# First weight quarter of each batch as two halves in rows of 4 KB, in place of three pieces by chunk; eleven identity matmuls in place of nine

## The chip, the core and the metric

The kernel runs on one core of one Trainium2 chip. A core has TensorE (PE in the profile, with its weight loads shown apart as PEld), VectorE (DVE), ScalarE (ACT), GpSimd (POOL) and SyncE (SP), an on-chip memory of 128 partitions, and PSUM, the memory into which TensorE writes. The metric is the device time of one execution in microseconds (us), taken as the median of several runs. All data here is float32; a float32 matmul appears in the profile as two records, and so does an identity matmul.

## The reference

For each of eight batches, x (256 tokens by 1024) is multiplied with one of eight weight matrices, chosen by an index; the product y goes through a base layer and a routed low-rank layer, and x is added:

```python
y      = einsum('bsi,boi->bso', x, weight[adapter_ids])
base   = einsum('btd,od->bto', y, base_W) + base_b
probs  = softmax(einsum('btd,nd->btn', y, router_W) + router_b)
p, i   = top_k(probs, 8)
w      = sum of p over the chosen rows by expert_map[i]
h      = einsum('btd,erd->bter', y, A)
out    = x + base + einsum('bter,eor->bto', h * w, B) * 2.0
```

## The kernel before

The work has two phases. **Phase one** computes y batch by batch. The 1024 by 1024 weight is split in four quarters of 512 by 512 (1 MB each): a11, a12, a21, a22. Seven quarter products, made from the quarters and from sums and differences of them, take the place of eight. Each quarter product is a `block` of 16 matmuls: four output tiles m by four contraction chunks k of 128. **Phase two** does the same with the base layer over groups of four batches; the change leaves it alone.

A quarter lies on the chip as a tile "wt" of 128 partitions, 4 chunks k, 512 outputs: 8 KB a partition. There are eight such buffers (`wpool`, line 65), shared by the quarters, their sums and later operands.

`load(b)` (line 284) fetches batch b. For b = 0, x comes in two transfers of 512 KB on ACT's queue (line 302). All weights go on SP's queue, in program order: the adapter index is read into a register (line 307), then a11 in **three pieces** (lines 310 to 318): chunk 0 (256 KB), chunk 1 (256 KB), chunks 2 and 3 (512 KB). They come from a DRAM tensor of its own, `w11`, in which the host has laid each piece as one contiguous block, so that a row (one partition's contiguous run) is 2 KB in the first two pieces and 4 KB in the third. Then `load_w` (line 289) fetches a12, a22 and a21 from `wq`, where a quarter is stored as two contiguous halves of 512 KB with rows of 4 KB: for b = 0 in two transfers each (`parts = 2`), for later batches in one transfer of 1 MB.

The order on PE, DVE, ACT and SP is the order of the program text (`manual_schedule`). At the start PE runs nine identity matmuls (lines 363 to 365), which read nothing but a constant. DVE makes four differences of x (`turns`), then the sums of the weight quarters: s1 = a21 + a22 in two halves (line 342), s2 = s1 - a11 (347), s4 = a12 - s2 (350), a11 - a21 (351). PE runs the blocks of batch 0 in the order a11, a12, a22, s1, s2, s4, a11 - a21. For b = 0 the first five blocks go through their matmuls chunk by chunk (`k_outer`): all four m of k = 0, then of k = 1, and so on, so a block can begin when chunk 0 has landed. For b of 1 and more, `load(b + 1)` is issued at the top of batch b, and its blocks run one batch later. Each transfer into a wt buffer waits on SP until the buffer's earlier readers are done.

The accumulators of the first three blocks are called pa (a11), pb (a12) and, second buffer of the same name, pb again (a22); pc takes s1.

Of the kernel before, what the change touches and what calls it, by code (L numbers as in the profile page):

```python
# [10 lines left out]
F32 = mybir.dt.float32  # L11
# [17 lines left out]
def kernel(  # L29
# [3 lines left out]
    xq: bass.AP,  # L33
    xr: bass.AP,
    ids: bass.AP,
    w11: bass.AP,

    wq: bass.AP,
    bq: bass.AP,
    base_b: bass.AP,  # L40
# [6 lines left out]
    nc = tc.nc  # L47
    P = 128
# [2 lines left out]
    KC = 8  # L51
    KH = 4
    OH = 512
    NA = w11.shape[0]
    N = emap.shape[1]
    ER = bT.shape[0]
    E = (N + 1) // 2
# [7 lines left out]
    wpool = ctx.enter_context(tc.tile_pool(name="w", bufs=8))  # L65
# [141 lines left out]
    with ExitStack() as phase:  # L207
# [76 lines left out]
        def load(b):  # L284

            x = xpool.tile([P, 2, 2, KH, P], F32, name="x")
            q = {}

            def load_w(name, i, parts=1):
                q[name] = wpool.tile([P, KH, OH], F32, name="wt")  # L290
                t = q[name].rearrange("p (h k) o -> p h (k o)", h=2)
                for n in range(parts):
                    h = ts(n, 2 // parts)
                    nc.sync.dma_start(
                        t[:, h],
                        wq[ds(adapter, 1), i, h].rearrange("e h p f -> p (e h) f"),
                    )

            if b == 0:

                for j in range(2):
                    nc.scalar.dma_start(
                        x[:, j].rearrange("p i k t -> p (i k t)"), x0[j]
                    )
            else:
                nc.sync.dma_start(x.rearrange("p j i k t -> p (j i k t)"), xq[b - 1])
            adapter = nc.sync.value_load(
                ids_sb[0:1, b : b + 1], min_val=0, max_val=NA - 1
            )
            q["a11"] = wpool.tile([P, KH, OH], F32, name="wt")  # L310

            for k, n in ((0, 1), (1, 1), (2, 2)):
                nc.sync.dma_start(
                    q["a11"][:, ds(k, n)].rearrange("p k o -> p (k o)"),
                    w11[ds(adapter, 1), ds(k * P * OH, n * P * OH)].rearrange(
                        "e (p f) -> p (e f)", p=P
                    ),
                )
            parts = 2 if b == 0 else 1
            load_w("a12", 0, parts)  # L320
            load_w("a22", 2, parts)
            load_w("a21", 1, parts)
            return x, q

        def turns(x):
# [18 lines left out]
        def other_sums(q):  # L344
# [13 lines left out]
            tc.manual_schedule(engines={EN.PE, EN.DVE, EN.Activation, EN.SP})  # L358
        )
        x, q = load(0)  # L360
        first = q

        idle = ps_t.tile([P, S], F32, name="pt")
        for _ in range(9):
            nc.tensor.matmul(idle[:, :P], lhsT=ident, rhs=ident, start=True, stop=True)
        t1, t2, t4 = turns(x)
        first_sum(q)
# [2 lines left out]
        for b in range(B):  # L370
# [6 lines left out]
            if not last:  # L377
                x, nq = load(b + 1)
# [52 lines left out]
            if not last:  # L431
                other_sums(nq)
                q, t1, t2, t4 = nq, nt1, nt2, nt4
# [343 lines left out]
```

## Time and profile before

| what | value |
|---|---|
| median of 3 runs | 443.89 us (443.81 to 443.92) |
| the profiled execution | 442.66 us |
| its span, first to last instruction | 440.9 us |
| PE busy in the span | 434.5 us (99%), 2994 matmul records |
| DVE busy | 303.2 us (69%) |
| DMA traffic | 106.19 MB, mean 241 GB/s |
| granted TensorE clock | 1.00 in every stretch asked for |

The span runs from the first to the last instruction of the program; 1.76 us of the profiled execution lie outside it. Times inside the trace are in us from the span's start. PE's busy time is modelled from pipelined matmuls; the start times of its records are the sharper view.

The transfers that open the span, each with the time of its issue and of the semaphore update that tells of its landing, as the trace has them:

| transfer | KB | row | queue | issued | landed | after the landing before |
|---|---|---|---|---|---|---|
| x, first half | 512 | 4 KB | ACT | 0.74 | 4.05 | |
| x, second half | 512 | 4 KB | ACT | 1.15 | 5.31 | 1.27 |
| a11, chunk 0 | 256 | 2 KB | SP | 2.93 | 5.99 | |
| a11, chunk 1 | 256 | 2 KB | SP | 3.52 | 6.65 | 0.66 |
| a11, chunks 2 and 3 | 512 | 4 KB | SP | 4.05 | 8.79 | 2.15 |
| a12, first half | 512 | 4 KB | SP | 4.57 | 10.35 | 1.56 |
| a12, second half | 512 | 4 KB | SP | 5.31 | 11.64 | 1.29 |
| a22, first half | 512 | 4 KB | SP | 5.84 | 12.92 | 1.28 |
| a22, second half | 512 | 4 KB | SP | 6.36 | not shown | |
| a21, first half | 512 | 4 KB | SP | 7.08 | 15.48 | |
| a21, second half | 512 | 4 KB | SP | 7.68 | 16.74 | 1.26 |

In later batches the same three pieces of a11 appear with these landings: batch 1 20.77, 21.43, 22.69; batch 3 64.04, 64.67, 67.24; batch 4 93.08, 93.73, 96.40; batch 6 180.55, 181.28, 183.65.

### The profile page before, as it was taken

To read this page: it belongs to the slowest core of one execution; us is meant where nothing else is said; L and a number is where in the kernel's file an instruction comes from. 1 tells how busy PE (TensorE), PEld (TensorE's weight loads), DVE (VectorE), ACT (ScalarE), POOL (GpSimd) and SP (SyncE) were. 2 spreads that over 40 slices of the span, in tenths; PEclk is the share of its full clock that TensorE was granted. 3 is DMA by queue.
4 is the path that set the end of the run, shared out by engine and by line. 5 is a ranking of instruction groups with operands and counts; after the bars stand their busy time and mean duration, and the time that the engine had idled before them with its cause. 6 is when DMAs were issued, how large, how long until landed. Compare 5 with 4: busy or idle time off the path is not lost.

```text
span 440.9 us, 7299 instructions
## 1 busy us (share of the span) xinstructions
PE 434.5 (99%) x2994; PEld 409.7 (93%) x2994; DVE 303.2 (69%) x516; ACT 40.4 (9%) x89; POOL 0.7 (0%) x6
## 2 busy tenths in 40 slices
PE   7999999999999999999999999999999999999997
PEld 6999999999999999999999888888888888888886
DVE  2579695682963967939629957755597858755594
ACT  1101111011011110110111200000200200000200
POOL 0000000000000000000000000000000000000000
PEclk9999999999999999999999999999999999999999
DMA  8989879678597797893370956821967726921843
GB/s 303 407 348 349 313 273 273 219 282 308 181 284 274 240 290 266 266 315 143 134 297 0 371 226 238 337 115 37 354 249 261 277 89 214 371 83 53 306 153 133
DMA packets 34050, 106.19 MB, mean 241 GB/s; under 512 B 3298, under 2 KB 7138, under 8 KB 30818
## 3 DMA queue, kind: packets, MB, share of 16 engines
q1 hardware_dynamic: 33730, 104.69, 67.0%
q10 hardware_dynamic: 288, 1.05, 0.6%
q8 instruction: 23, 0.38, 0.3%
q14 instruction: 9, 0.07, 0.0%
HBM read 84.49 MB, written 21.23 MB: 240 GB/s over the span
## 4 chain that ended last, share of the span: by engine, by line
PE 92%; DVE 5%; DMA 1%; issue 1%; SPq 0%
PE pa L243 24%; PE pa L478 20%; PE pc L243 12%; PE pc L478 10%; PE pb L243 7%; PE ph L107 6%; PE pb L478 5%; PE pc L487 3%; PE pb L487 2%; PE pa L487 1%; DMA wt<-in_w_dram 1%; DVE tt L186 1%; PE pe L478 1%; DVE y L630 0%; PE pt L203 0%
## 5 line engine op out<-in xcount | busy, mean ns | idle before, releaser
L478 PE MATMUL pa<-tt,wt 128*128 128x256 f32 x324 | 78.0, 379 | 0.1
L478 PEld LDWEIGHTS pa<-tt,wt 128*128 128x128 f32 x324 | 61.4, 190 | 8.9 <-DVE u L508 0.5
L243 PE MATMUL pa<-x,wt 128*128 128x128 f32 x512 | 59.9, 275 | 1.8 <-DMA wt<-in_w_dram 1.8
L243 PEld LDWEIGHTS pa<-x,wt 128*128 128x128 f32 x512 | 58.5, 192 | 2.2 <-issue 1.3
L243 PE MATMUL pa<-tt,wt 128*128 128x128 f32 x480 | 56.0, 275 | 0.0
L243 PEld LDWEIGHTS pa<-tt,wt 128*128 128x128 f32 x480 | 54.8, 192 | 0.0
L116 DVE TENSOR_TENSOR lg<-ph,rb 128x30 f32<-128x30 f32 x8 | 1.5, 189 | 49.9 <-ACT h L115 49.9
L107 PE MATMUL ph<-ar_sb,y 128*128 128x143 f32 x256 | 32.7, 284 | 0.0
L107 PEld LDWEIGHTS ph<-ar_sb,y 128*128 128x128 f32 x256 | 31.8, 190 | 0.0
L243 PE MATMUL pc<-tt,wt 128*128 128x128 f32 x256 | 29.9, 275 | 0.0
L243 PE MATMUL pc<-x,wt 128*128 128x128 f32 x256 | 29.9, 275 | 0.0
L243 PE MATMUL pb<-x,wt 128*128 128x128 f32 x256 | 29.9, 275 | 0.0
L243 PEld LDWEIGHTS pc<-tt,wt 128*128 128x128 f32 x256 | 29.2, 192 | 0.0
L243 PEld LDWEIGHTS pc<-x,wt 128*128 128x128 f32 x256 | 29.2, 192 | 0.0
L243 PEld LDWEIGHTS pb<-x,wt 128*128 128x128 f32 x256 | 29.2, 192 | 0.0
L478 PE MATMUL pc<-tt,wt 128*128 128x256 f32 x112 | 27.8, 379 | 0.0
L342 DVE TENSOR_TENSOR wt<-wt 128x2048 f32<-128x2048 f32 (+1 forms) x9 | 18.5, 2051 | 10.2 <-DMA wt<-in_wq_dram 10.2
L478 PE MATMUL pc<-y,wt 128*128 128x256 f32 x96 | 24.0, 379 | 0.0
L478 PE MATMUL pb<-y,wt 128*128 128x256 f32 x96 | 24.0, 379 | 0.0
L478 PEld LDWEIGHTS pc<-tt,wt 128*128 128x128 f32 x112 | 21.2, 190 | 3.0
L478 PE MATMUL pa<-y,wt 128*128 128x256 f32 x92 | 21.9, 379 | 0.0
L601 DVE TENSOR_TENSOR q<-q,xt 128x512 f32<-128x512 f32 x31 | 21.3, 686 | 0.5
(117 smaller groups left out, 488.0 us busy)
## 6 DMA issues: line engine op xcount, KB each, us to landing
wt<-in_wq_dram SPq DMA_DIRECT2D x21, 1024.0 KB, 6.1
wt<-left_raw SPq DMA_DIRECT2D x14, 1024.0 KB, 5.5
wt<-left_sum SPq DMA_DIRECT2D x14, 768.0 KB, 8.0
xt<-in_xr_dram SPq DMA_DIRECT2D x32, 256.0 KB, 6.8
out_dram<-q SPq DMA_DIRECT2D x31, 256.0 KB, 2.3
x<-in_xq_dram SPq DMA_DIRECT2D x7, 1024.0 KB, 4.9
wt<-in_w_dram SPq DMA_DIRECT2D x16, 256.0 KB, 2.8
wt<-in_w_dram SPq DMA_DIRECT2D x8, 512.0 KB, 4.9
```

Of the source, the lines that this page charges most:

```text
L107: nc.tensor.matmul(ph[:, j], lhsT=y[:, k // KH, th, k % KH // 2, bi, k % 2, ts(j, P)], rhs=ar_sb[:, k, :], start=(j == order[0] and k == 0 ...
L116: nc.vector.tensor_add(lg, ph[:, :, ER:], rb.unsqueeze(1).to_broadcast([P, NTT, N]))
L186: nc.vector.tensor_sub(t[n], x, y)
L243: nc.tensor.matmul(acc[:, m // 2, m % 2, :], lhsT=left[:, k, ts(m, P)], rhs=right[:, k, :], start=(first and n == 0), stop=(k == KH - 1), ...
L342: nc.vector.tensor_add(q["s1"][:, h], q["a21"][:, h], q["a22"][:, h])
L478: nc.tensor.matmul(acc[mi][:, mi, :], lhsT=left[:, 2 * k + mi, :], rhs=right[:, k, :], start=(first and k == 0 and (mi == 0 or acc[0] is n ...
L487: nc.tensor.matmul(acc[mi][:, mi, :], lhsT=up[:, ts(mi, P)], rhs=hw, start=False, stop=True, skip_group_check=True,)
L601: add(q, q, x)
```

## The change

The tensor `w11` is gone. `wq` holds four quarters instead of three, all as two halves in rows of 4 KB, and a11 is loaded by `load_w` like the others: for batch 0 as two transfers of 512 KB, for each later batch as one of 1 MB. The bytes are the same. Nine identity matmuls become eleven. On the host side only the layout of the inputs changes.

```diff
-    NA = w11.shape[0]
+    NA = wq.shape[0]
...
-            q["a11"] = wpool.tile([P, KH, OH], F32, name="wt")
-
-            for k, n in ((0, 1), (1, 1), (2, 2)):
-                nc.sync.dma_start(
-                    q["a11"][:, ds(k, n)].rearrange("p k o -> p (k o)"),
-                    w11[ds(adapter, 1), ds(k * P * OH, n * P * OH)].rearrange(
-                        "e (p f) -> p (e f)", p=P
-                    ),
-                )
             parts = 2 if b == 0 else 1
-            load_w("a12", 0, parts)
-            load_w("a22", 2, parts)
-            load_w("a21", 1, parts)
+            load_w("a11", 0, parts)
+            load_w("a12", 1, parts)
+            load_w("a22", 3, parts)
+            load_w("a21", 2, parts)
...
-        for _ in range(9):
+        for _ in range(11):
             nc.tensor.matmul(idle[:, :P], lhsT=ident, rhs=ident, start=True, stop=True)
```

More of the change, by code (lines that the diff above doesn't have):

```diff
@@ L35 @@
     ids: bass.AP,
-    w11: bass.AP,
     wq: bass.AP,
@@ L740 @@
         "ids": a["itok_B_3_7"].reshape(1, nb),
-        "w11": _np.concatenate(
-            [w[:, 0, :2].reshape(len(w), -1)]
-            + [w[:, 0, 2:].transpose(0, 2, 1, 3).reshape(len(w), -1)],
-            axis=1,
-        ),
-        "wq": w[:, 1:]
-        .reshape(-1, 3, 2, d // 512, 128, d // 2)
+        "wq": w.reshape(-1, 4, 2, d // 512, 128, d // 2)
         .transpose(0, 1, 2, 4, 3, 5)
-        .reshape(-1, 3, 2, 128, d // 512 * (d // 2)),
+        .reshape(-1, 4, 2, 128, d // 512 * (d // 2)),
         "bq": base.reshape(4, 128, -1),
```

## The prediction

> **What bounds the kernel now.** I read the chain that ended last first, then what PE waited for, then the opening of PE's and SP's timelines, then each transfer's landing. The shares of the chain by engine, from the page:
>
> ```profile
> PE 92%; DVE 5%; DMA 1%; issue 1%; SPq 0%
> ```
>
> PE is the bound nearly everywhere. Everything PE ever waited for, over the whole span (us in total, times, longest):
>
> ```profile
> PE pa L243 <- DMA wt<-in_w_dram: 1.8, 2, 1.1
> PE pt L365 <- POOL ident masks.py:199: 1.4, 1, 1.4
> ```
>
> So the only waits that this change can touch are two, on pieces of a11. PE's timeline from 0 to 26 us (start, duration; the bracket is idle time before it) shows both:
>
> ```profile
> 1.36 3.63 PE L365 MATMUL pt<-ident 128*128 128x128 f32 x18 [1.36 <-POOL ident masks.py:199]
> 6.12 2.02 PE L243 MATMUL pa<-x,wt 128*128 128x128 f32 x16 [1.13 <-DMA wt<-in_w_dram]
> 8.84 2.05 PE L243 MATMUL pa<-x,wt 128*128 128x128 f32 x16 [0.69 <-DMA wt<-in_w_dram]
> 10.73 3.74 PE L243 MATMUL pb<-x,wt 128*128 128x128 f32 x32
> 14.30 3.74 PE L243 MATMUL pb<-tt,wt 128*128 128x128 f32 x32
> 17.87 3.74 PE L243 MATMUL pc<-tt,wt 128*128 128x128 f32 x32
> ```
>
> The identity matmuls end at 4.99, chunk 0 starts at 6.12, chunks 0 and 1 run through, then PE is idle 0.69 us until the third piece is there at 8.79. From 8.84 it never stops: the three starts after 10.73 lie 3.57 us apart, 32 records at 0.112. What counts is therefore one number, **the start of the second block (pb, a12), 10.73 now**; any shift of it moves the end by as much, unless a later wait appears. SP's timeline says when the transfers are issued:
>
> ```profile
> 2.93 1.46 SPq L313 DMA_DIRECT2D wt<-in_w_dram  x3
> 4.57 3.61 SPq L294 DMA_DIRECT2D wt<-in_wq_dram  x6
> ```
>
> **The two halves of batch 0.** Three issues on SP become two, and the followers are issued some 0.5 us sooner (2.93, 3.52, 4.05, 4.57 are the present steps). That by itself gains nothing: the trace's DMA packets show the first packet of a11 at 4.57, 1.6 us after its issue, when x's last packets (until about 4.9) still ran, and the engines stay full afterwards. The stream of bytes sets the landings, not SP.
>
> Half 1 is chunks 0 and 1 in one semaphore: 512 KB. Its bytes are those of the first two pieces, which had landed at 6.65. Per DMA engine they were 16 packets of 2 KB at 84 ns (1.34 us) and become 8 of 4 KB at 159 ns (1.27 us): 0.07 less, so 6.57. [...]
>
> [...] Five packets of the third piece took 0.76 to 1.18 us each; it landed 2.15 us after the second, where the later halves take 1.28. So the time of half 1 is the unknown cost, and rows for it are:
> - the a22 and second a12 halves: 1.28, no stall. Half 1 at 6.57.
> - a12's first half, the same form by the same line as the new half 1, the first of its tile: 1.56, a stall of 0.28. Half 1 at 6.85.
> - the third piece, the first in 4 KB rows on SP's queue: 2.15, a stall of 0.87. Half 1 at 7.44.
> - the third piece in batch 4 (93.73 to 96.40): 2.67, a stall of 1.39. Half 1 at 7.96.
>
> From there, PE: 0.13 us from landing to the first record (5.99 to 6.12), 16 records to chunk 2 in 1.86 (7.87 + 0.11 - 6.12), 16 more in 1.79 without a new start, 1.89 with one (10.73 - 8.84). I take a12's first half, the nearest in form and line: start 6.85 + 0.13 = 6.98, chunk 2 at 8.84. Half 2, at a12's second half's 1.29, lands at 8.14 and is not waited for; **pb starts at 8.84 + 1.79 = 10.63, 0.10 earlier**. If instead half 1 is clean and half 2 has the third piece's stall, half 2 lands at 6.57 + 2.15 = 8.72, PE restarts at 8.77, pb at 10.66: 0.07 earlier. Two distributions of one stall, the same answer: what PE loses by starting later (6.98 for 6.12) it had been losing anyway in the 0.69 us gap. Clean throughout: 6.70, 8.56, pb at 10.35: 0.38 earlier. That is about the most that can be won, since half 1 cannot land much before 6.57.
>
> Next in line behind it: a12's first half lands at 10.35 today and would now land at 8.14 + 1.28 = 9.4 to 10.35, before PE wants it in every case. DVE's s2 ends at 20.38 and is wanted at 21.45, s1's first half about 16.8 for 17.87: 1.07 us of room, more than the 0.38 that PE can come sooner.
>
> **The two added identity matmuls** are four records at 0.112 (the spacing from 4.27 on; before that it was 0.213): PE is done with them at 4.99 + 0.45 = 5.44, before 6.57. They cost nothing while half 1 lands after about 5.4, and cover part of the longer idle time: 6.98 - 5.44 = 1.54 us against 1.13 now. Would the matmuls slow down to the 0.213 spacing after such a pause? The row shows only that 1.13 us did not do it. From the row alone a longer pause could cost as much as the warm-up: 1.36 to 4.27 at 0.213 is 13.7 records, 1.4 us dearer than at 0.112. [...]
>
> **Later batches.** Seven times, three transfers become one of 1 MB, two SP issues fewer (0.53 us each). Hidden: batch 3's pieces land at 67.24 and are first read at 86.87 (DVE's s2) and 90.25 (PE). 20 us of cover, for a transfer that takes 5 to 6 us. Behind them on SP the next issue (64.86) waits for a block of PE, not for the queue. Should the 1 MB land 1 us later, the transfers after it have the same kind of slack. Zero.
>
> **Sum**: -0.10 us on the profiled execution, 442.66 to 442.56. The median of the runs lies 1.23 above it; the same shift on 443.89 gives **443.8**. About 0.2% (0.89 us) is what a measurement of this kernel can tell from no change.
>
> **Rivals.**
> 1. Clean stream, both halves at 1.28: -0.38, 443.5. For it: the five halves after a12's first run so. Against: each stream of 4 KB rows began with slow packets, x's too (eight of about 0.5 us). Still within 0.2%.
> 2. The stall moves wholly into half 1 at the third piece's size: 7.44, 7.57, 9.43, pb at 11.22: +0.49, 444.4. For it: half 1 is now the first in 4 KB rows on SP's queue. Against: it follows x, whose rows are 4 KB too, so the stream may be settled already. Within 0.2%.
> 3. Slower: the same mechanism at batch 4's size: half 1 at 7.96, PE 8.09, pb at 11.74: +1.01, 444.9. It decides from a landing of half 1 at 7.83 on (7.83 + 0.13 + 1.86 + 1.79 = 11.61, 0.89 late). Before, a stall behind chunks 0 and 1 was partly hidden by their 1.86 us of matmuls; a stall in half 1 has no work to hide behind. A clock that falls back in the pause would bring 2 to the same side. Against: the runs of before lie within 0.11 us of each other, so the opening is no lottery, and its own stall was 0.87.
> 4. Faster by over 0.2% would need pb at 9.84, half 1 at 6.05: 0.5 us sooner than its bytes can come. Only something outside the span could do it.
>
> **Chances**: the forecast (a stall of about 0.3 in half 1, or all in half 2) 0.45; rival 1 0.18; rival 2 0.20; rival 3 0.13; faster than 0.2% 0.04. So faster 0.04, same 0.83, slower 0.13. The range for 8 in 10 holds the first three cases with 0.2 to 0.3 for the runs: 443.3 to 444.6.
>
> **What would show it.** In the trace of after: one landing for half 1 near 6.6 to 6.9 and PE's first a11 record 0.13 later; all 32 a11 records without a gap (forecast), or with a gap before chunk 2 (the other distribution); 22 identity records ending near 5.4 with 0.112 spacing at the first real ones; pb near 10.6; no new wait of PE after it. The prediction is wrong if half 1 lands after 7.8, if the first a11 records are 0.213 apart, or if PE shows a wait in a later batch.

## The result, and the profile after

In the comparison of the two kernels, 20 runs each, the median fell from 443.75 to **442.78 us**; the ratio is 0.9983, with a 95% interval of 0.9976 to 0.9990. Three later comparisons, on three different chips, gave 0.9976 (0.9966 to 0.9986), 0.9984 (0.9976 to 0.9992) and 0.9981 (0.9971 to 0.9990). The medians differ by 0.97 us; the ratio follows the means, 443.66 and 442.91, and stands for a gain of 0.75 us. The 442.78 us lie below the predicted range of 443.3 to 444.6.

The profile after does not show it: that execution took 444.51 us, the longest of its 20, with a span of 442.7. Its chain of waits and what PE waited for, as shown for before:

```profile
PE 93%; DVE 5%; DMA 1%; issue 1%; SPq 0%
```

```profile
PE pa L241 <- DMA wt<-in_wq_dram: 1.9, 1, 1.9
PE pt L355 <- POOL ident masks.py:199: 1.4, 1, 1.4
```

PE's timeline from 0 to 20 us (lines 355 and 241 are 365 and 243 of before):

```profile
1.36 4.20 PE L355 MATMUL pt<-ident 128*128 128x128 f32 x22 [1.36 <-POOL ident masks.py:199]
7.42 5.44 PE L241 MATMUL pa<-x,wt 128*128 128x128 f32 x32 [1.86 <-DMA wt<-in_wq_dram]
12.69 3.74 PE L241 MATMUL pb<-x,wt 128*128 128x128 f32 x32
```

Half 1 landed at 7.28 and PE paused 1.86 us, longer than before; the gap ahead of chunk 2 is gone. But the 32 records of a11 took 5.44 us in place of some 3.7, and pb starts at 12.69. The view by stretches says why (stretch and length in us; busy time and count of PE, PEld, DVE, ACT and POOL; granted clock, DMA share, GB/s):

```profile
4.48:7.89 3.41, 1.55 (x14) 1.39 (x13) 1.71 (x3) 0.00 (x0) 0.00 (x0) 1.00 0.97 376
7.89:11.31 3.42, 3.42 (x18) 3.42 (x18) 0.97 (x2) 0.00 (x0) 0.00 (x0) 0.50 1.01 393
```

The clock records of the trace change at 4.481, 7.894 and 11.308, 3.413 us apart. In the first of these windows PE was busy 1.55 of 3.41 us, 45%; in the next it was granted half the clock, and only 18 records ran: about half of 3.41 us, 1.7, was lost. A usual execution of the changed kernel was profiled in a later experiment (442.96 us, span 441.2):

```profile
1.36 4.51 PE L355 MATMUL pt<-ident 128*128 128x128 f32 x22 [1.36 <-POOL ident masks.py:199]
6.71 2.02 PE L241 MATMUL pa<-x,wt 128*128 128x128 f32 x16 [0.83 <-DMA wt<-in_wq_dram]
9.15 2.05 PE L241 MATMUL pa<-x,wt 128*128 128x128 f32 x16 [0.41 <-DMA wt<-in_wq_dram]
11.03 3.74 PE L241 MATMUL pb<-x,wt 128*128 128x128 f32 x32
```

Here pb starts at 11.03, no earlier than in the profiled execution of before (10.73). So the question for the experiments was not what the change shortens, but **what the usual execution of before loses that its profiled one did not**. The profiled one took 442.66 us; the median was 443.75.

### The profile page after: what moved, and what is told of

It is laid out like the page before. It is cut to its first block, busy times and chain, and to the rows that moved or that the text cites. A ratio compares the mean times of both kernels' runs of the same rounds, so it can differ in the third digit from the quotient of the medians.

```text
span 442.7 us, 7249 instructions
## 1 busy us (share of the span) xinstructions
PE 436.4 (99%) x2998; PEld 411.8 (93%) x2998; DVE 303.1 (68%) x516; ACT 40.3 (9%) x89; POOL 0.7 (0%) x6
## 4 chain that ended last, share of the span: by engine, by line
PE 93%; DVE 5%; DMA 1%; issue 1%; SPq 0%
PE pa L241 25%; PE pa L468 20%; PE pc L241 12%; PE pc L468 10%; PE pb L241 7%; PE ph L105 6%; PE pb L468 5%; PE pc L477 3%; PE pb L477 2%; PE pa L477 1%; DMA wt<-in_wq_dram 1%; DVE tt L184 1%; PE pe L468 1%; DVE y L620 0%; PE pt L201 0%
## 5 line engine op out<-in xcount | busy, mean ns | idle before, releaser
L241 PE MATMUL pa<-x,wt 128*128 128x128 f32 x512 | 61.3, 280 | 1.9 <-DMA wt<-in_wq_dram 1.9
L241 PEld LDWEIGHTS pa<-x,wt 128*128 128x128 f32 x512 | 60.0, 196 | 2.0 <-issue 2.0
```

The costliest lines, as they stand in the source:

```text
L241: nc.tensor.matmul(acc[:, m // 2, m % 2, :], lhsT=left[:, k, ts(m, P)], rhs=right[:, k, :], start=(first and n == 0), stop=(k == KH - 1), ...
```

## The experiments

All kernels with their comparison; "over 443.5" counts the runs above that time. The line was drawn after seeing the runs, in the gap between the two groups that halves with nine matmuls fell into.

| a11 of batch 0 | identity matmuls | median us (runs) | over 443.5 | ratio (95%) |
|---|---|---|---|---|
| three pieces (before; six sets) | 9 | 443.64 to 443.88 (236) | 180 | 1 |
| three pieces (before, a seventh set) | 9 | 443.65 (14) | 11 | 0.9999 (0.9987 to 1.0011) |
| two halves (the change; four sets) | 11 | 442.78, 443.07, 442.81, 442.94 (73) | 5 | above |
| three pieces | 11 | 443.30 (14), 443.88 (14) | 6, 11 | 0.9998 (0.9988 to 1.0008), 1.0003 (0.9994 to 1.0013) |
| two halves | 9 | 443.51 (14), 443.85 (14) | 7, 8 | 1.0003 (0.9992 to 1.0015), 1.0002 (0.9987 to 1.0016) |
| two halves | 16 | 443.17 (14) | 4 | 0.9997 (0.9988 to 1.0006) |
| three pieces | 14 | 443.72 (14) | 9 | 1.0004 (0.9995 to 1.0013) |
| two halves | 4 | 445.15 (21) | 21 | 1.0022 (1.0012 to 1.0031) |
| two halves | 30 | 445.79 (5) | 5 | 1.0038 (1.0025 to 1.0052) |
| three pieces, 1 MB later | 9 | 444.17 (13) | 11 | 1.0005 (0.9993 to 1.0017) |
| three pieces, same tensor | 11 | 443.29 (21) | 9 | 0.9990 (0.9983 to 0.9996) |
| two halves, own tensor | 11 | 443.31 (21) | 8 | 0.9991 (0.9984 to 0.9998) |
| two halves, x's second half later | 9 | 443.55 (14) | 8 | 0.9994 (0.9982 to 1.0005) |
| four pieces of 2 KB rows | 11 | 442.54 (6), 442.82 (14) | 0, 1 | 0.9969 (0.9957 to 0.9981), 0.9979 (0.9970 to 0.9989) |

**One part at a time, and more cover.** Eleven matmuls with the three pieces:

```diff
-        for _ in range(9):
+        for _ in range(11):
```

> The kernel before with eleven identity matmuls in place of nine; a11 stays in three pieces. Theory A (TensorE's clock: the typical run of before falls to half clock for a stretch because PE was idle too long between the identity matmuls and the end of a11, and four more identity records keep it up): the whole gain appears here, 442.7 to 443.0 us, 0.7 to 1.0 under before. Theory B (transfers: in the typical run the third piece lands about 1 us later than in the profiled one, and the halves mend it): no gain, 443.6 to 443.9, clock 1.0 in before too.

Halves with nine:

```diff
-        for _ in range(11):
+        for _ in range(9):
```

> The changed kernel with nine identity matmuls; a11 in halves. Theory A: PE's pause grows (to about 2 us or more), so more runs fall to half clock: 443.7 or slower, up to 444.5, with clock means of 0.996 to 0.999 in many runs. Theory B: the halves alone carry the gain: 442.7 to 443.0.

Neither theory holds: neither part gains anything that the interval can tell. Halves with nine fell in two groups, seven runs at 442.65 to 443.03 and seven at 443.99 to 444.51; the second group is as slow as theory A had said. But only one of those seven had a mean clock below 1 (0.996). Since the clock column knows nothing of the time before its first record (in the profile of before it reads 1.00 from 0.83 to 4.24 us, where the records are 0.213 apart), a full clock that is granted late leaves it at 1.00, and that became the next question. Sixteen matmuls with halves, and fourteen with pieces (`range(16)`, `range(14)`):

> The changed kernel with sixteen identity matmuls: 32 records, some 13 at 0.213 us and the rest at 0.112, so PE is busy until about 6.6 and hardly pauses before half 1 lands. Theory A: no run falls to half clock, the spread narrows, none near 444.5, median 442.4 to 442.8. Theory B: as with eleven, 442.7 to 443.0, outliers stay. If half 1 lands before 6.5 in most runs, both lose 0.1 to 0.2 for it.

> The kernel before with fourteen identity matmuls: busy until about 6.1, when chunk 0 lands. Theory A: as e1 or better, 442.5 to 442.9, clock 1.0. Theory B: 443.6 to 443.9.

More cover alone does not help either. With pieces, 9 of 14 runs stay above 443.5 with fourteen matmuls (443.72, as theory B had it): what makes them late is not the pause ahead of a11. Sixteen with halves missed both theories (443.17) and leave 4 of 14; an estimate of why: where the full clock comes late, 32 records at 0.213 would last until 8.2 us and hold a11 up themselves. Its profile (full clock at 5.25) cannot show that.

**The clock by itself.** The changed kernel with thirty and with four identity matmuls, beside the changed kernel again:

> The changed kernel itself, on the chip of the first four experiments. If the 0.17% of the first comparison is the change's: 442.8 to 443.0 and a ratio near 0.998. If it belongs to the draw of the runs or to the chip: 443.1 to 443.5, ratio 0.999 to 1.000, and a spread of about 2 us as in the four experiments before.

> The changed kernel with thirty identity matmuls: 60 records, PE busy until 9.5 to 11 us, so all of a11 and a12's first half have landed before PE wants them, and no pause is left. The runs of every version so far spread over some 2 us. Theory C (that spread is the clock: the moment at which the full clock is granted differs from run to run, some 4.2 to 7.6 us): the spread stays, 1 to 1.6 us, flat, since each record before that moment costs 0.10 us more; times 445.0 to 446.6. Theory D (the spread is in the landings of a11): it goes, all runs within 0.4 us.

> The changed kernel with four identity matmuls: PE is idle from about 3.1 to 6.6. Theory C: every run begins a11 at half clock, and the full clock comes one window of about 3.4 us later: 444.3 to 445.5, first a11 records 0.213 apart. Theory D, or a clock that does not depend on the identity matmuls: 442.8 to 443.5.

The changed kernel repeated its gain (443.07 beside 443.88 of before). Four matmuls cost some 2 us against it, as theory C had it. The profile of that kernel (445.38 us):

```profile
1.36 2.07 PE L355 MATMUL pt<-ident 128*128 128x128 f32 x8 [1.36 <-POOL ident masks.py:199]
7.08 6.41 PE L241 MATMUL pa<-x,wt 128*128 128x128 f32 x32 [3.65 <-DMA wt<-in_wq_dram]
```

The a11 records took 6.41 us, 24 of them at the spacing of 0.213, and the first clock record stands at 12.53. With thirty, five runs lay within 0.6 us, between what C (1 to 1.6) and D (0.4) had said: undecided. Its profile had the full clock from 6.82 on, the profiles before from 4.24 to 5.25: the moment does move.

**Later batches alone.** Batch 0 as before, a11 of batches 1 to 7 in one transfer:

```diff
-            q["a11"] = wpool.tile([P, KH, OH], F32, name="wt")
-
-            for k, n in ((0, 1), (1, 1), (2, 2)):
+            if b == 0:
+                q["a11"] = wpool.tile([P, KH, OH], F32, name="wt")
+            else:
+                load_w("a11", 0)
+            for k, n in ((0, 1), (1, 1), (2, 2)) if b == 0 else ():
...
```

> The kernel before, with batch 0 in three pieces and nine identity matmuls, but a11 of batches 1 to 7 as one transfer of 1 MB. My step says hidden: no difference, 443.4 to 443.8, ratio 0.9995 to 1.0005, no new wait of PE. Rival: SP's fewer issues or the wider rows help phase one: 442.8 to 443.0.

No gain. Its profile (445.18 us) caught what the pieces can do:

```profile
6.38 2.02 PE L243 MATMUL pa<-x,wt 128*128 128x128 f32 x16 [0.81 <-DMA wt<-in_w_dram]
10.70 2.05 PE L243 MATMUL pa<-x,wt 128*128 128x128 f32 x16 [2.30 <-DMA wt<-in_w_dram]
12.59 0.61 PE L243 MATMUL pb<-x,wt 128*128 128x128 f32 x4
```

The third piece landed at 10.66, 3.77 us after the second (8.79 and 2.15 in the profile of before). PE also had one wait of 0.3 us in phase two, for left_raw. Four profiles of the changed kernel, whose later transfers are the same, show no such wait.

**All four combinations on one chip.** The theory with two causes was then set against either alone:

> The changed kernel beside its two halves and the kernel before on one chip. Theory H (two causes: the identity matmuls keep the clock from being granted a window late, worth 0.3 to 0.6 us of the median; the halves take away the late third piece, worth another 0.3): 442.8 to 443.1, ratio 0.9975 to 0.9985, best of the four. Theory G (identity matmuls alone): equal to the pieces with eleven, 443.2 to 443.4.

> Three pieces, eleven identity matmuls. Theory H: 443.2 to 443.5, between the changed kernel and the one before; where the profile is of a slow run, the third piece has landed after 9.3 and PE waits for it, with the full clock. Theory G: equal to the changed kernel. Theory E (halves alone): equal to the kernel before.

> Halves, nine identity matmuls. Theory H: two groups of runs again, one near 442.8 (clock granted in time) and one near 444.3 (granted one window later, or fallen): where the profile is of the second group, a11's records are 0.213 apart at pb's start after 12. Theory E: equal to the changed kernel, one group.

> The kernel before once more, for a profile of one of its usual runs (443.5 to 444.2; the profile read so far is of one of its fastest, 442.66). Theory H: pb starts near 12.0, late either because a11's records run at 0.213 until 9.5 or later (full clock granted after a11 has begun) or because the third piece lands near 10; the trace says which. Ratio 1.000.

Medians of 442.81, 443.88, 443.85 and 443.65, with 1 of 22, 11 of 14, 8 of 14 and 11 of 14 runs over 443.5. Two causes, but the shares do not add up as theory H had put them: neither part alone gives a gain that its interval can tell, both together give the whole. The profiles show why. A usual execution of before, 443.89 us:

```profile
1.36 4.21 PE L365 MATMUL pt<-ident 128*128 128x128 f32 x18 [1.36 <-POOL ident masks.py:199]
6.23 5.82 PE L243 MATMUL pa<-x,wt 128*128 128x128 f32 x32 [0.66 <-DMA wt<-in_w_dram]
11.89 3.74 PE L243 MATMUL pb<-x,wt 128*128 128x128 f32 x32
```

```profile
8.00:10.00 2.00, 2.00 (x12) 2.00 (x11) 0.26 (x1) 0.00 (x0) 0.00 (x0) 1.00 0.93 365
...
12.00:14.00 2.00, 2.00 (x20) 2.00 (x19) 0.00 (x0) 0.59 (x1) 0.00 (x0) 1.00 1.03 424
```

PE never waited after 6.23 (the third piece had landed at 9.28, before it was wanted), yet a11 took 5.82 us: 12 records in two us against 20 later on. The column says 1.00 throughout, because the first clock record is at 10.46. The nine matmuls had lasted until 5.57, a11 began at 6.23, and in the 3.42 us that, counted back from 10.46 by 3.41, ended at 7.05 PE was busy for 2.76, 81%; the full clock was not granted then, but at 10.46, 3.41 us later. In the profile of before with 442.66 us, PE was busy 2.88 of the 3.41 us that ended at 4.24 (84%), and there the full clock was granted. The two stretches, the usual execution first:

```profile
3.63:7.05 3.42, 2.76 (x14) 2.50 (x13) 1.47 (x3) 0.00 (x0) 0.00 (x0) 1.00 1.05 385
```

```profile
0.83:4.24 3.41, 2.88 (x13) 2.88 (x14) 0.00 (x0) 1.28 (x1) 0.41 (x2) 1.00 0.71 258
```

How often this happens is an estimate from these two stretches alone: the full clock came after the one with 0.54 us of idle time and not after the one with 0.66. It assumes a line at 0.6 between them, and windows of 3.41 us ahead of the first clock record too; no run shows either. Nine matmuls at half clock end at 5.57, so a window that ended between about 6.2 and 7.6 would hold more idle time than that; for one that ended later, the window before it would hold less. That is 1.4 of 3.41 us, two runs in five if every edge is equally likely. Eleven at half clock end at 6.43 (as in the profile of four pieces, below), close to the landing of half 1 (6.48 to 7.28 in ten profiles with halves), and by the same estimate seldom leave such a pause.

And three pieces with eleven matmuls, 443.65 us:

```profile
6.04 2.02 PE L243 MATMUL pa<-x,wt 128*128 128x128 f32 x16
9.84 2.05 PE L243 MATMUL pa<-x,wt 128*128 128x128 f32 x16 [1.78 <-DMA wt<-in_w_dram]
11.73 3.74 PE L243 MATMUL pb<-x,wt 128*128 128x128 f32 x32
```

Here the full clock came at 5.72, a11 began without any pause, and the third piece landed at 9.80: 1.78 us of waiting at full clock. So two different accidents, each seen in a profile, end at the same place, pb near 11.8, and **one of them is enough**. Pieces with eleven were over 443.5 in 17 of 28 runs (61%), halves with nine in 15 of 28 (54%). If the two accidents were independent, before should be there in 1 - 0.39 x 0.46 = 82% of its runs; it was in 180 of 236, 76%. With both removed, 5 of 73 remain. The late group of halves with nine was not caught in a profile (that one took 442.98). That it is the clock is inferred: the kernel differs from the changed one only in two identity matmuls, which touch no transfer, and 13 of its 15 late runs have a mean clock of 1.00, as a late grant leaves it; the other two have 0.996, as in the profile after, where the clock fell.

**Rows or tensor.** What makes the third piece late? Three pieces cut out of the common tensor, and halves in a tensor of their own, both with eleven matmuls:

```diff
-            load_w("a11", 0, parts)
+            for k, n in ((0, 1), (1, 1), (2, 2)):
...
+                    wq[ds(adapter, 1), 0, k // 2, :, ds(k % 2 * OH, n * OH)].rearrange(
...
```

> The changed kernel (eleven identity matmuls, a11 in the same tensor and layout as the other quarters), but a11 again fetched in three pieces: chunk 0, chunk 1 (runs of 2 KB out of rows of 4 KB), then half 2. Theory E (the third piece behind two pieces of 2 KB runs lands late in about half of the runs, as in the profile of the later-batches experiment, 10.65 us against 9.0 to 9.3 for half 2): slow like eleven matmuls with pieces, 443.2 to 443.7, runs up to 444.5. Theory F (the place of the separate tensor in memory does it): 442.8 to 443.1, like the change. Theory G (identity matmuls alone do it): 442.8 to 443.1 too.

```diff
-            for k, n in ((0, 1), (1, 1), (2, 2)):
+            for k, n in ((0, 2), (2, 2)):
```

> The kernel before with eleven identity matmuls and a11 in a tensor of its own, but laid in two halves with rows of 4 KB (two transfers in every batch). Theory E: 442.8 to 443.1, as the change, no run above 443.5 except one whose clock fell. Theory F: 443.2 to 443.7, runs up to 444.5.

443.29 is what E had said and 443.31 what F had said, so neither alone explains it. Each gains about half of what the change does (0.9990 and 0.9991, both intervals below 1) and leaves 9 and 8 of 21 runs over 443.5, so rows of 4 KB alone do not remove the late runs. The changed kernel itself was not run beside them. In the profile of the halves in their own tensor (443.68 us) half 2 landed at 9.51 and PE restarted at 9.55. What decides when the second half of a11 lands (8.32 to 10.66 us in the profiles, 7.45 in that of the next version) stays open.

**Two versions meant to beat both.** First, x's second half, called between the two halves of a12, and nine identity matmuls:

```diff
-                for j in range(2):
-                    nc.scalar.dma_start(
-                        x[:, j].rearrange("p i k t -> p (i k t)"), x0[j]
-                    )
+                def half(engine, j):
+                    engine.dma_start(x[:, j].rearrange("p i k t -> p (i k t)"), x0[j])
+
+                half(nc.scalar, 0)
...
-            load_w("a12", 1, parts)
+            load_w("a12", 1, parts, (lambda: half(nc.sync, 1)) if b == 0 else None)
```

> A version meant to beat both: as the change, but x's second half, which only the differences of x read, goes on SP's queue behind a12's first half instead of ahead of a11; nine identity matmuls. Half 1 should land some 1.2 us sooner, about 5.3 to 5.7, and PE then runs with what the byte stream allows (a12's second half and t4 become due about when they land): pb at 9.8 to 10.4 instead of about 11, 441.9 to 442.4. If the stream only moves the wait to a12's second half, t4 or s1, 442.7 to 443.1 with a new wait of PE there.

It missed, with 443.55. Half 1 landed at 6.17, 0.4 us sooner and not 1.2, all of a11 by 7.45, but a12's first half only at 10.36:

```profile
6.31 3.81 PE L241 MATMUL pa<-x,wt 128*128 128x128 f32 x32 [1.24 <-DMA wt<-in_wq_dram]
10.41 2.05 PE L241 MATMUL pb<-x,wt 128*128 128x128 f32 x16 [0.29 <-DMA wt<-in_wq_dram]
13.06 2.05 PE L241 MATMUL pb<-x,wt 128*128 128x128 f32 x16 [0.60 <-DMA wt<-in_wq_dram]
```

The stall only fell on the next tile, and PE gained two new waits. Second, all of a11 by chunk:

```diff
-            for k, n in ((0, 1), (1, 1), (2, 2)):
+            for k, n in ((0, 1), (1, 1), (2, 1), (3, 1)):
```

> The kernel before with eleven identity matmuls and a11 in four pieces by chunk, all in rows of 2 KB. Theory E in the form 'a change from rows of 2 KB to rows of 4 KB brings the late landing': a11 lands by 8.0, the late landing moves to a12's first half, wanted at about 9.8 to 10: PE waits there, 443.0 to 443.6. In the form 'the second half MB of a11 stalls whatever its rows': as with three pieces, 443.2 to 443.7, PE waiting for the third or fourth piece until 9 or later. If rows of 2 KB never stall: 442.3 to 442.7.

Six runs, 442.30 to 442.69. No form of E had that; "rows of 2 KB never stall" had the time but not the reason, for packets of 2 KB took up to 0.87 us here. The chunks landed at 6.05, 6.99, 8.11 and 9.15, each before PE wanted it, though the full clock came only at 7.40:

```profile
6.22 4.36 PE L243 MATMUL pa<-x,wt 128*128 128x128 f32 x32
10.53 3.84 PE L243 MATMUL pb<-x,wt 128*128 128x128 f32 x32
```

Again, beside the changed kernel on one chip:

> a11 in four pieces of 256 KB by chunk, rows of 2 KB, eleven identity matmuls, beside the changed kernel on one chip. If the six tight runs of the first time (442.30 to 442.69) are the kernel's: 442.4 to 442.7, all within 0.6 us, 0.2 to 0.4 under the changed kernel, since PE waits for single chunks and the stall around 6 to 8 us holds up one of them, not two. If they were a lucky draw: spread up to 444 as with three pieces, 443.3 or more.

> The changed kernel beside it: 442.8 to 443.1, ratio to the kernel before 0.9975 to 0.9985.

442.82 and 442.94, with overlapping intervals (0.9979 and 0.9981 to before); one run took 444.11. Four pieces beat the kernel before; that they beat the changed one is not shown. They do show that a11 can come in time without halves and without rows of 4 KB.

## Why the prediction was wrong

- **PE is the bound, and only the start of pb counts: right.** Span less pb's start is 430.2 us before, 430.1 in the profile after, 430.2 in the usual run of before and 430.1 for pieces with eleven.
- **The failing step is the carry-over to the median.** The prediction said: "The median of the runs lies 1.23 above it; the same shift on 443.89 gives 443.8." It took that difference for something outside the argument. Time less span is 1.76 to 1.92 us in all twenty profiles; the difference lay inside the span, in the very stretch under study: pb at 10.73 in the profiled execution, at 11.89 in the usual one. Usual against usual, the change moves pb from 11.89 to 11.03, 0.86 us, and not by the forecast 0.10. For the same reason rival 4 saw no way to a larger gain: against the profiled execution there is hardly any, and the best run of the changed kernel in the first comparison (442.43) is only 0.23 below 442.66. The change makes the usual run nearly as good as the best.
- **"The opening is no lottery": wrong.** Three runs within 0.11 us were too few, and the profiled execution, 1.2 us below them, was a fourth that spoke against it; 236 runs of before reach from 442.07 to 446.81.
- **The two identity matmuls at no effect: wrong.** They hold off a full clock that comes 3.41 us late (10.46 for 7.05 in the usual run of before), one of the two accidents. The sum also has nothing for a clock that falls back in the longer pause, and no run shows that nothing. In the profile after, the clock fell to 0.50 after a pause of 1.86 us, with PE busy 45% of the 3.41 us between clock records, and some 1.7 us were lost: the 1.4 us that the prediction read from the row alone was nearer. In a profile of halves with nine, with a pause of 1.75 us and PE busy 1.66 of 3.41 us (49%), the clock stayed.
- **Half 1 at 6.85: right in size.** Ten profiles with halves have 6.48 to 7.28. The reason was wrong: the prediction had slow packets where a stream of 4 KB rows begins, but in the profile after a11's rows of 4 KB began at 4.60 and its two slowest packets, 0.50 and 0.68 us, at 7.99 and 7.35, and with four pieces those of 2 KB took up to 0.87 us. **Half 2 at 8.14, or 8.72 with the third piece's stall: the second, and more.** They have 8.57 to 9.51, and in five of them PE waits there, 0.17 to 0.70 us. So pb, forecast at 10.63, started at 10.60, 11.03, 11.23 and 12.69 in the four profiles of the changed kernel.
- **Later batches at zero: right**, within the interval of that experiment, 0.9993 to 1.0017.
- **One reading was off without effect.** The trace has a11's first packet at 4.62, not 4.57.

## What to carry to other kernels

One profile is one execution: before a gain is summed against it, ask whether it is a usual one, and when its time lies away from the median, look for the difference inside the stretch that is to be changed. A kernel can have two accidents that lead to the same lateness; then each remedy alone can measure as nothing, and only the pair (or a table of all four combinations) shows what they are worth. The identity matmuls had a price on both sides here: with too few the full clock came late (at 12.53 with four, 445.15 us; at 10.46 in a usual run with nine), and with thirty they delayed the real work (a11 from 10.75 on, 445.79 us).

## What the runs showed of the hardware

- In the profile after TensorE's granted clock changes at 4.481, 7.894 and 11.308 us, 3.413 apart; in the profile of before the one grant lasts 436.906 us, 128 times as long. The first clock record differs from run to run: it was seen at 4.24 to 7.40 us, at 10.46 in a usual run of before, and at 12.53 with four identity matmuls. The full clock was granted after 3.41 us in which PE was busy 84% (before, until 4.24), and not after 81% (the usual run of before, until 7.05) and 60% (four identity matmuls, 2.04 of 3.42, until 9.12). Once granted, it stayed with 49% (halves with nine, 1.66 of 3.41) and fell with 45% (after, 1.55 of 3.41). These shares rest on PE's modelled busy time and on one stretch each; where between them the clock would change was not shown. The clock column shows nothing before the first grant; the spacing of records does: in the profile of before 0.213 us until 4.24 and 0.112 from 4.27 on.
- In the first 18 us of the profile of before, packets of the weight stream took 0.084 us with 2 KB and mostly 0.159 with 4 KB; none of 2 KB took longer, but eight of 4 KB took 0.69 to 1.18 us, beginning between 6.03 and 8.26. In the profile after, two of 4 KB took 0.50 and 0.68 us, beginning at 7.99 and 7.35. With four pieces, packets of 2 KB took up to 0.87 us. What causes it was not found.
